# Joining plain loads in a planned graph kernel: adjacency in pairs of tiles, masks once, rows of several lists together

## The chip, the cores and the metric

The kernel runs on one core of one Trainium2 chip. The metric is the device time of one execution in microseconds (us). The kernel before has four runs, and one more execution was taken with the hardware profiler, whose lines are shown below.

## The reference, cut to what matters

There are 16 graphs ("batches") of 1024 nodes with 64 channels, a weighted adjacency of 1024 x 1024 per graph, and a node mask. Layer 0 is a normalised matrix product. Layer 1 takes, for each node and channel, a weighted sum of three quantiles over its neighbours, after some neighbours have been dropped, and then a small MLP.

```python
# layer 0
h = jnp.maximum(_layernorm(x), 0.0)
deg = jnp.clip(jnp.sum(adj, axis=2, keepdims=True), 1.0, None)
x = x + jnp.matmul(adj / deg, h)
# layer 1
h = jnp.maximum(_layernorm(x), 0.0)
adj_d = _dilate_adj(adj, nodemask)           # drops every skip-th neighbour of nodes with more than 10
agg = _weighted_nanquantile_agg(h, adj_d > 0) # 0.25, 0.5, 0.75 with weights 0.25, 0.5, 0.25
hid = jax.nn.relu((h + agg) @ W1 + b1)
x = x + (hid @ W2 + b2) * nodemask[..., None]
```

The adjacency is sparse and very uneven: a few nodes have up to some 88 neighbours, most have five or fewer. A quantile needs the neighbours' values sorted, per channel.

## The kernel before, in words

**Engines and what they do.** PE (TensorE) transposes and multiplies, ACT (ScalarE) copies out of PSUM, makes signs and normalises, DVE (VectorE) finds neighbours and sorts, POOL (GpSimd) issues indirect gathers and scatters, SP (SyncE) issues the plain transfers, in the order in which they are written to its queue.

**First part, per batch.** `loads` (line 570) has SP load the batch's `x` into `xt`, its mask into `mrow`, and its adjacency in eight tiles of 128 rows into `at` (five buffers). `signs` (610) turns a tile into fp16 signs `sg` on ACT, and `listing` has DVE multiply them by descending column numbers and take the eight largest of each of four segments (MAX8 into `rec`): these are the neighbours' numbers. `transposes` turns the same tile on PE, ACT copies it to `att`, and `products` multiplies `att` with the normalised `h0`. `beginnings` (588) makes `h0`, and writes the node number and mask into the last two columns of `row`. `channels` makes layer 1's normalised values and stores them to the table `tab` in DRAM (SP). `endings` ranks the batch's nodes by their degree, and POOL scatters each node's `row` (own values, residual, neighbour list, node, mask: 164 numbers) to `srt`, so that nodes of like degree lie together.

**Second part, per group of four batches.** `group` reads the sorted lists back (`recs`), drops neighbours, and starts a `Job` (841) for each class of list length. There are ten classes for 31 tiles of nodes: lengths 15, 10, 8, 7 (two tiles), 6, and then 5, 4, 3, 2 and 1 with four to six tiles each. A job has POOL gather the neighbours' rows one list place at a time into `places`, SP load the nodes' own rows into `S` (four buffers), DVE sort by a network of minima and maxima between `places` and `other`, and then, in `layers` (1099), PE, ACT and DVE run the MLP into `y` (six buffers). SP loads the residual into `y` first; POOL scatters the result to the output.

**Third part, long lists.** `long_lists` (1299) takes the 128 nodes at each of the first four ranks (lists of up to 88, 31, 24 and 20), one per partition. SP loads their own rows into `lS`, four loads per list, one for each group.

**What sets the order.** All of these are generators that yield the engine they need next and the time from which they can go on. `Plan` holds a clock for each engine and for the transfers, estimates when each tile is ready and when a buffer is free (`room(name, bufs)`), and always runs the entry that can begin first; ties and priorities come from a rank. A change of a buffer count or of a transfer thus changes the order of everything behind it. Every instruction that goes through the plan has the line 238 in the profile, so that groups are told apart by their tiles. A further path for dense graphs follows the list path; it doesn't run on this input.

Of the kernel before, what the change touches and what calls it, by code (L numbers as in the profile page):

```python
# [243 lines left out]
class Plan:  # L244
# [25 lines left out]
    def room(self, name, bufs):  # L270

        tiles = self.slots.get(name, ())
        if len(tiles) < bufs:
            return 0.0
        old = tiles[-bufs]
        return INF if self.users[old] else max(self.used.get(old, 0.0), self.ready.get(old, 0.0))

    def at(self, *tiles):
        return max(self.ready.get(t.tensor.name, INF) for t in tiles)
# [104 lines left out]
def list_path(ctx, tc, x, adj, nodemask, w1, b1, w2, b2, out, go):  # L384
# [93 lines left out]
    wt0 = consts.tile([P, 1], F32, name="wt0")  # L478
    nc.vector.memset(wt0, QUANTILES[0][1])

    before = consts.tile([P, NT], F32, name="before")
    nc.vector.tensor_scalar(before, col_f[:, :NT], -float(P), None, op0=OP.mult)

# [82 lines left out]
    def known(st, *names):  # L566

        return max(at(st[name]) if name in st else INF for name in names)

    def loads(pool, now):  # L570
        def nodes(st, b):
            yield "SP", lambda: room("xt", 3)
            st["xt"] = new(pool, [P, NT, C], F32, "xt", 3, users=1)
            nc.sync.dma_start(st["xt"], x[b].rearrange("(t p) c -> p t c", p=P))
            st["mrow"] = new(tiny, [NT, P], U8, "mrow", 3)
            nc.sync.dma_start(st["mrow"], nodemask[b].rearrange("(t p) -> t p", p=P))

        yield from nodes(batch[0], 0)
        for b, st in enumerate(batch):
            now[0] = b  # L580
            for t in range(NT):
                if t == 2 and b + 1 < B:
                    yield from nodes(batch[b + 1], b + 1)
                yield "SP", lambda: room("at", 5)
                st["rows"][t] = new(pool, [P, N], F32, "at", 5, users=2)
                nc.sync.dma_start(st["rows"][t], adj[b, t * P:(t + 1) * P, :])

    def beginnings(pool, now):

        for b, st in enumerate(batch):  # L590
            now[0] = b
            yield "DVE", lambda: max(known(st, "xt", "mrow"), room("h0", 3), room("row", 4))
            mrow_f = new(tiny, [NT, P], F32, "mrow_f", 2)
            nc.vector.tensor_copy(mrow_f, st["mrow"])

            h0 = new(pool, [P, NT, C + 1], F32, "h0", 3, users=2)
            nc.vector.memset(h0[:, :, C:], 1.0)
            row = st["row"] = new(pool, [P, NT, RW], F32, "row", 4, users=1)
            nc.vector.memset(row[:, :, C:W], -1.0)
            yield from normed(h0[:, :, :C], st["xt"])  # L600
            st["h0"] = h0
            yield "PE", lambda: max(at(mrow_f), room("ps_small", 3))
            pm = new(ps_s, [P, HALF], F32, "ps_small", 3, users=1)
            nc.tensor.transpose(pm[:, :NT], mrow_f, ident[:NT, :NT])
            yield "ACT", lambda: at(pm)
            nc.scalar.copy(row[:, :, RW - 1], pm[:, :NT])
            nc.scalar.copy(row[:, :, RW - 2], row_f)
            free(pm)

    def signs(pool, now):  # L610
        for b, st in enumerate(batch):
            now[0] = b
            for t in range(NT):
                yield "ACT", lambda: max(
                    at(st["rows"][t]) if t in st["rows"] else INF, room("sg", 4),
                    0.0 if t else room("total", 4),
                )
                if t == 0:
                    st["total"] = new(tiny, [P, NT], F32, "total", 4, users=1)
                sg = new(pool, [P, N], HF, "sg", 4, users=1)  # L620
                nc.scalar.activation(
                    sg, st["rows"][t], AF.Sign, accum_out=st["total"][:, t:t + 1]
                )
                st["signs"][t] = sg
                free(st["rows"][t])
# [202 lines left out]
    def scatter(dst, src, idx, others):  # L828
# [9 lines left out]
        others.append(ins.ins)  # L838
        plan.last = others

    class Job:

        def __init__(self, pool, n, T, keys, idx, node, mask, nodes_i, table, S, g, name="places",
                     bufs=4, rank=0, half=False, begin=0.0):
            self.__dict__.update(locals())
            self.short = pool is gat
            self.tag = "" if self.short else "l0" if name == "lplaces0" else "l"
            self.block = BLOCK if self.tag == "l0" else n  # L850
            self.bufs1 = 1 if self.tag == "l0" else 2

        def run(self):
            n, T, pool, short = self.n, self.T, self.pool, self.short

            since = []
            own = () if short else (lambda rank: self.rank,)
            pace = lambda: since[0] + 1.3 * len(since) if not short else 0.0
            yield "POOL", lambda: max(
                self.begin, at(self.idx), room(self.name, self.bufs), room("S", 4) if short else 0.0  # L860
            ), *own
            A = self.A = new(pool, [P, n, T, W], F32, self.name, self.bufs, users=1)
            progress["ahead"] += T * (n - 1)
            parts = self.parts() if self.block < n else None
            if short:
                mine = self.S
                self.S = new(pool, [P, T, C], F32, "S", 4, users=1)
                nc.sync.dma_start(self.S, mine[:, :, :C])
                self.residual = mine[:, :, X1:R0]
            for t in range(T):  # L870
                for k in range(n - 1):
                    if t or k:
                        yield "POOL", pace, *own
                    since.append(since[0] if since else plan.clock["POOL"])
                    plan.own = plan.clock["POOL"]
                    gather(A[:, k + 1, t, :], self.table, self.idx[:, t, k:k + 1])
                    plan.own = None
                    progress["ahead"] -= 1
                    if parts and ((k + 2) % self.block == 0 or k == n - 2):
                        plan.add(parts(), self.rank)  # L880
            if parts:
                yield "DVE", lambda: self.landed if self.left == 0 else INF, self.soon
                yield from self.merge()
                return
            yield "DVE", lambda: max(
                at(A, self.S) + SLACK,
                *(room(self.tag + name, self.bufs1) for name in ("gone", "wu")),
            ), self.soon
            yield from self.sort()
# [209 lines left out]
        def layers(self, terms, sources):  # L1099

            T, R = self.T, terms[0][0].shape[1]
            yield "PE", lambda: max(at(*sources) + LOOSE, room("y", 6), room("pt", 2))
            y = new(mlp, [P, T, CO], F32, "y", 6, users=1)
            x1 = y
            if self.short:
                nc.sync.dma_start(x1, self.residual)
            else:
                x1 = self.S[:, :, X1:R0]
            for t0 in range(0, T, 4):
                ts = range(t0, min(t0 + 4, T))  # L1110
# [51 lines left out]
    def group(g, kept=grp, name=""):  # L1162
# [120 lines left out]
        for t in range(begin, NTAU):  # L1283
            if classes and caps[t] == caps[classes[-1][0]]:
                classes[-1].append(t)
            else:
                classes.append([t])
        for i, ts in enumerate(classes):
            n, T = caps[ts[0]] + 1, len(ts)
            sl = slice(ts[0], ts[-1] + 1)  # L1290
            job = Job(
                gat, n, T, keys[:, sl, :n - 1], idx[:, sl, :], node[:, sl], mask[:, sl],
                nodes_i[:, sl], table, tiles[:, sl, :R0], g,
                half=0 in ts, begin=dropped,
            )
            plan.add(job.run(), 100 * g + i)
        progress["groups"] = g + 1

    def long_lists(pool):

        yield "DVE", always
        rev = new(pool, [P, N], HF, "rev", 1)
        nc.vector.tensor_scalar(rev, col_f, -1.0, float(N), op0=OP.mult, op1=OP.add)
        for l in LORDER:
            K = LONG[l]
            n = K + 1
            yield "SP", always
            S = new(pool, [P, 1, RW], F32, "lS", 4)
            for g in range(NG):
                lo, num = FIRST[g] * LSUB, GROUPS[g] * LSUB  # L1310
                at0 = l * num + (0 if GROUPS[g] == 4 else HP)
                nc.sync.dma_start(
                    S[lo:lo + num, 0, :], srt[g][at0:at0 + num, :]
                )
            node = S[:, 0, RW - 2:RW - 1]
            mask = S[:, 0, RW - 1:RW]
            yield "DVE", lambda: at(S) + SLACK if progress["begun"] == NG else INF
# [377 lines left out]
```

## Time and profile before

| | us |
|---|---|
| median of four runs | 1907.45 |
| the four runs | 1901.99, 1930.16, 1892.49, 1912.90 |
| the profiled execution's own time | 1901.99 |
| its span from the first to the last instruction | 1899.9 |
| DVE busy / POOL busy / PE busy | 1269.7 / 964.8 / 811.9 |
| PE weight loads / ACT busy | 505.8 / 580.0 |

The mean granted clock of TensorE was 0.642 of full speed. In a line of instructions the columns are start, duration, engine, source line, operation, tile written and read, count. In a line of waits they are: who waited, for whom, us in total, how many times, longest. The profile has 16 DMA engines on which the transfers of all queues run; the adjacency is 128 loads of 512 KB, `S` and `y` are 40 loads each, `lS` 16 of 20.5 KB, the mask 16 of 1 KB.

### The profile page before, as it was taken

What the parts mean: (1) busy time and instruction counts of PE and PEld (TensorE: products, weight loads), DVE (VectorE), ACT (ScalarE), POOL (GpSimd) and SP (SyncE); (2) the same over time, 40 slices, a digit from 0 to 9 for tenths busy, and PEclk for the clock granted to TensorE, in tenths of its full rate; (3) what the DMA queues carried; (4) which work ended last, traced back from release to release, by engine and by line L of the source; (5) the groups of instructions that cost most, each with busy time, mean ns of one, the idle gap of its engine ahead of it and who ended that gap; (6) DMA issues with size and microseconds to landing.
All of it is one profiled execution on the core that took longest, in us unless ns stands there. A gap on an engine that the chain in (4) does not pass through costs nothing.

```text
span 1899.9 us, 14970 instructions
## 1 busy us (share of the span) xinstructions
PE 811.9 (43%) x3192; PEld 505.8 (27%) x3192; DVE 1269.7 (67%) x4220; ACT 580.0 (31%) x1746; POOL 964.8 (51%) x1154
## 2 busy tenths in 40 slices
PE   5777743336646435466732643101002003332346
PEld 3333322214423313233422321101001003332334
DVE  7766845958565557457746855778887359695773
ACT  7987743326513313364342341000000000010001
POOL 0123156373455363625667455566787743716654
PEclk8887866565766566677755876555555555765556
DMA  5545644224433212334331222211111100101110
GB/s 163 162 122 148 188 108 109 75 42 113 111 82 78 54 41 74 90 113 105 107 97 47 62 50 52 57 42 43 26 23 25 26 15 9 29 11 37 32 23 15
DMA packets 135710, 133.28 MB, mean 70 GB/s; under 512 B 100756, under 2 KB 103444, under 8 KB 135492
## 3 DMA queue, kind: packets, MB, share of 16 engines
q1 hardware_dynamic: 102876, 90.79, 17.4%
q0 software_dynamic: 32736, 41.47, 9.9%
q14 instruction: 71, 0.58, 0.1%
q8 instruction: 27, 0.44, 0.1%
HBM read 112.90 MB, written 23.61 MB: 72 GB/s over the span
## 4 chain that ended last, share of the span: by engine, by line
DVE 42%; another core or an unknown queue 15%; issue 13%; PE 11%; ACT 11%; DMA 5%; POOL 2%; SPq 0%; DVEq 0%; POOLq 0%; ACTq 0%
PE ps_small L238 6%; DVE places L238 6%; DVE other L238 6%; DVE lplaces L238 5%; PE pt L238 5%; DVE l0other L238 3%; DMA at<-in_adj_dram 3%; ACT sg L238 3%; ACT ln_sq L238 3%; DVE rec L238 2%; ACT att L238 2%; DVE lfound L238 2%; DVE lkey L238 2%; DVE lother L238 2%
## 5 line engine op out<-in xcount | busy, mean ns | idle before, releaser
L238 POOL DMA_INDIRECT places<-tab,idx x372 | 365.8, 983 | 168.8 <-issue 109.1
L238 PE MATMUL pt<-ident,prod 128*128 128x128 f32 (+1 forms) x736 | 165.4, 389 | 528.5 <-DVE prod L238 479.2
L238 PE MATMUL pt<-ident,at 128*128 128x128 f32 x1024 | 200.7, 349 | 268.4 <-issue 127.6
L238 PE MATMUL ps_small<-att,h 128*65 128x512 f32 x512 | 265.7, 670 | 42.7 <-ACT h L238 19.6
L238 PEld LDWEIGHTS pt<-ident,prod 128*128 128x128 f32 (+1 forms) x736 | 134.0, 269 | 562.0 <-issue 337.4
L238 POOL DMA_INDIRECT srt<-row,to x128 | 128.1, 1000 | 285.1 <-ACT row L238 263.5
L238 PEld LDWEIGHTS pt<-ident,at 128*128 128x128 f32 x1024 | 152.4, 179 | 320.8 <-issue 166.6
L238 ACT COPY att<-pt 128x512 f32<-128x512 f32 x256 | 144.3, 582 | 251.0 <-remote 137.1
L238 POOL DMA_INDIRECT lplaces<-whole,lidx x163 | 168.1, 1031 | 49.7 <-issue 49.4
L238 DVE MAX8 rec<-sg 128x8 f16<-128x256 f16 x512 | 180.1, 414 | 8.1 <-remote 2.7
L238 POOL DMA_INDIRECT out_dram<-y,nodes_i x93 | 100.0, 1075 | 156.5 <-DVE y L238 81.5
L238 ACT COPY ot<-pt 128x128 f32<-128x128 f32 (+3 forms) x56 | 22.3, 398 | 447.9 <-PE pt L238 225.8
L238 POOL DMA_INDIRECT places<-tab,last_idx x124 | 123.7, 998 | 53.9 <-issue 36.9
L238 ACT ACTIVATE sg<-at 128x1024 f16<-128x1024 f32 x128 | 134.8, 1054 | 43.9 <-DMA at<-in_adj_dram 23.5
L238 DVE TENSOR_TENSOR sg<-sg,keyed 128x1024 f16<-128x1024 f16 x128 | 87.5, 683 | 73.3 <-ACT sg L238 65.1
L238 PEld LDWEIGHTS ps_small<-att,h 128*65 128x65 f32 x512 | 77.9, 158 | 188.3 <-issue 145.2
L238 PE MATMUL ps_small<-ot,w_sb 128*128 128x128 f32 (+3 forms) x112 | 58.0, 612 | 132.9 <-ACT ot L238 73.0
L238 DVE TENSOR_TENSOR other<-places,other 128x64 f32<-128x64 f32 (+6 forms) x204 | 69.5, 341 | 41.1 <-remote 17.0
L238 DVE TENSOR_TENSOR places<-places,other 128x64 f32<-128x64 f32 (+2 forms) x208 | 62.3, 309 | 22.3 <-remote 7.6
L238 ACT ACTIVATE wu<-wu 128x39 f32<-128x39 f32 (+9 forms) x40 | 9.3, 234 | 197.7 <-DVE wu L238 167.4
L238 DVE TENSOR_TENSOR places<-other,places 128x128 f32<-128x128 f32 (+5 forms) x160 | 54.9, 343 | 19.0 <-DVE other L238 6.8
L238 DVE TENSOR_TENSOR other<-other,places 128x64 f32<-128x64 f32 (+3 forms) x156 | 50.1, 321 | 21.8 <-remote 6.6
(251 smaller groups left out, 1650.7 us busy)
## 6 DMA issues: line engine op xcount, KB each, us to landing
at<-in_adj_dram SPq DMA_DIRECT2D x128, 512.0 KB
places<-tab,idx POOLq DMA_INDIRECT x372
whole<-tab SPq DMA_DIRECT2D x4, 1057.0 KB
tab<-row SPq DMA_DIRECT2D x16, 264.0 KB
xt<-in_x_dram SPq DMA_DIRECT2D x16, 256.0 KB
lplaces<-whole,lidx POOLq DMA_INDIRECT x163
srt<-row,to POOLq DMA_INDIRECT x128
places<-tab,last_idx POOLq DMA_INDIRECT x124
```

Of the source, the lines that this page charges most:

```text
L238: ins = getattr(self._engine, op)(*args, **kwargs)
```

## The change

The adjacency is loaded in pairs of tiles into three buffers of two tiles (before: five of one tile). The masks of all batches are loaded and transposed once at the start, and node numbers and masks are kept in `marks`, from which one ACT copy per batch fills the two columns of `row`. The five classes with lists of more than 5 places (six tiles) share one load of `S` and one of `y`. The four long lists' own rows are loaded by four transfers, one for each group, instead of sixteen. To make room, `sg` has three buffers instead of four and `h0` two instead of three.

```diff
--- before.py
+++ after.py
@@ -478,6 +478,19 @@
     wt0 = consts.tile([P, 1], F32, name="wt0")
     nc.vector.memset(wt0, QUANTILES[0][1])
 
+    mrow = consts.tile([B * NT, P], U8, name="mrow")
+    nc.sync.dma_start(mrow, nodemask.rearrange("b (t p) -> (b t) p", p=P))
+    mrow_f = grp.tile([P, N], F32, name="gat_rows", bufs=1)[:B * NT, :P]
+    nc.vector.tensor_copy(mrow_f, mrow)
+    pm = ps_s.tile([P, HALF], F32, name="ps_small")
+    nc.tensor.transpose(pm[:, :B * NT], mrow_f, ident[:B * NT, :B * NT])
+    marks = consts.tile([P, B, NT, 2], HF, name="marks")
+    nc.vector.tensor_copy(
+        marks[:, :, :, 1].rearrange("p b t -> p (b t)"), pm[:, :B * NT]
+    )
+    nc.vector.tensor_copy(
+        marks[:, :, :, 0], row_f.unsqueeze(1).to_broadcast([P, B, NT])
+    )
     before = consts.tile([P, NT], F32, name="before")
     nc.vector.tensor_scalar(before, col_f[:, :NT], -float(P), None, op0=OP.mult)
 
@@ -572,8 +585,6 @@
             yield "SP", lambda: room("xt", 3)
             st["xt"] = new(pool, [P, NT, C], F32, "xt", 3, users=1)
             nc.sync.dma_start(st["xt"], x[b].rearrange("(t p) c -> p t c", p=P))
-            st["mrow"] = new(tiny, [NT, P], U8, "mrow", 3)
-            nc.sync.dma_start(st["mrow"], nodemask[b].rearrange("(t p) -> t p", p=P))
 
         yield from nodes(batch[0], 0)
         for b, st in enumerate(batch):
@@ -581,43 +592,39 @@
             for t in range(NT):
                 if t == 2 and b + 1 < B:
                     yield from nodes(batch[b + 1], b + 1)
-                yield "SP", lambda: room("at", 5)
-                st["rows"][t] = new(pool, [P, N], F32, "at", 5, users=2)
-                nc.sync.dma_start(st["rows"][t], adj[b, t * P:(t + 1) * P, :])
+                if t % 2 == 0:
+                    yield "SP", lambda: room("at", 3)
+                    pair = new(pool, [P, 2, N], F32, "at", 3, users=4)
+                    nc.sync.dma_start(
+                        pair, adj[b, t * P:(t + 2) * P, :].rearrange("(k p) j -> p k j", p=P)
+                    )
+                st["rows"][t] = pair[:, t % 2, :]
 
     def beginnings(pool, now):
 
         for b, st in enumerate(batch):
             now[0] = b
-            yield "DVE", lambda: max(known(st, "xt", "mrow"), room("h0", 3), room("row", 4))
-            mrow_f = new(tiny, [NT, P], F32, "mrow_f", 2)
-            nc.vector.tensor_copy(mrow_f, st["mrow"])
-
-            h0 = new(pool, [P, NT, C + 1], F32, "h0", 3, users=2)
+            yield "DVE", lambda: max(known(st, "xt"), room("h0", 2), room("row", 4))
+            h0 = new(pool, [P, NT, C + 1], F32, "h0", 2, users=2)
             nc.vector.memset(h0[:, :, C:], 1.0)
             row = st["row"] = new(pool, [P, NT, RW], F32, "row", 4, users=1)
             nc.vector.memset(row[:, :, C:W], -1.0)
             yield from normed(h0[:, :, :C], st["xt"])
             st["h0"] = h0
-            yield "PE", lambda: max(at(mrow_f), room("ps_small", 3))
-            pm = new(ps_s, [P, HALF], F32, "ps_small", 3, users=1)
-            nc.tensor.transpose(pm[:, :NT], mrow_f, ident[:NT, :NT])
-            yield "ACT", lambda: at(pm)
-            nc.scalar.copy(row[:, :, RW - 1], pm[:, :NT])
-            nc.scalar.copy(row[:, :, RW - 2], row_f)
-            free(pm)
+            yield "ACT", lambda: at(row)
+            nc.scalar.copy(row[:, :, RW - 2:], marks[:, b, :, :])
 
     def signs(pool, now):
         for b, st in enumerate(batch):
             now[0] = b
             for t in range(NT):
                 yield "ACT", lambda: max(
-                    at(st["rows"][t]) if t in st["rows"] else INF, room("sg", 4),
+                    at(st["rows"][t]) if t in st["rows"] else INF, room("sg", 3),
                     0.0 if t else room("total", 4),
                 )
                 if t == 0:
                     st["total"] = new(tiny, [P, NT], F32, "total", 4, users=1)
-                sg = new(pool, [P, N], HF, "sg", 4, users=1)
+                sg = new(pool, [P, N], HF, "sg", 3, users=1)
                 nc.scalar.activation(
                     sg, st["rows"][t], AF.Sign, accum_out=st["total"][:, t:t + 1]
                 )
@@ -838,12 +845,14 @@
         others.append(ins.ins)
         plan.last = others
 
+    mine_of = lambda share: share["rows"].shape[1]
+
     class Job:
 
 
 
         def __init__(self, pool, n, T, keys, idx, node, mask, nodes_i, table, S, g, name="places",
-                     bufs=4, rank=0, half=False, begin=0.0):
+                     bufs=4, rank=0, half=False, begin=0.0, shared=None, first=0):
             self.__dict__.update(locals())
             self.short = pool is gat
             self.tag = "" if self.short else "l0" if name == "lplaces0" else "l"
@@ -857,16 +866,23 @@
             own = () if short else (lambda rank: self.rank,)
             pace = lambda: since[0] + 1.3 * len(since) if not short else 0.0
             yield "POOL", lambda: max(
-                self.begin, at(self.idx), room(self.name, self.bufs), room("S", 4) if short else 0.0
+                self.begin, at(self.idx), room(self.name, self.bufs),
+                room("S", 4) if short and not (self.shared and "S" in self.shared) else 0.0,
             ), *own
             A = self.A = new(pool, [P, n, T, W], F32, self.name, self.bufs, users=1)
             progress["ahead"] += T * (n - 1)
             parts = self.parts() if self.block < n else None
             if short:
-                mine = self.S
-                self.S = new(pool, [P, T, C], F32, "S", 4, users=1)
-                nc.sync.dma_start(self.S, mine[:, :, :C])
-                self.residual = mine[:, :, X1:R0]
+                mine, share = self.S, self.shared
+                if share is None:
+                    share = {"users": 1, "rows": mine}
+                if "S" not in share:
+                    S = share["S"] = new(
+                        pool, [P, mine_of(share), C], F32, "S", 4, users=share["users"]
+                    )
+                    nc.sync.dma_start(S, share["rows"][:, :, :C])
+                self.share = share
+                self.S = share["S"][:, self.first:self.first + T, :]
             for t in range(T):
                 for k in range(n - 1):
                     if t or k:
@@ -1099,12 +1115,20 @@
         def layers(self, terms, sources):
 
             T, R = self.T, terms[0][0].shape[1]
-            yield "PE", lambda: max(at(*sources) + LOOSE, room("y", 6), room("pt", 2))
-            y = new(mlp, [P, T, CO], F32, "y", 6, users=1)
-            x1 = y
+            yield "PE", lambda: max(
+                at(*sources) + LOOSE, room("pt", 2),
+                0.0 if self.short and "y" in self.share else room("y", 6),
+            )
             if self.short:
-                nc.sync.dma_start(x1, self.residual)
+                share = self.share
+                if "y" not in share:
+                    y = share["y"] = new(
+                        mlp, [P, mine_of(share), CO], F32, "y", 6, users=share["users"]
+                    )
+                    nc.sync.dma_start(y, share["rows"][:, :, X1:R0])
+                y = x1 = share["y"][:, self.first:self.first + T, :]
             else:
+                y = new(mlp, [P, T, CO], F32, "y", 6, users=1)
                 x1 = self.S[:, :, X1:R0]
             for t0 in range(0, T, 4):
                 ts = range(t0, min(t0 + 4, T))
@@ -1285,6 +1309,9 @@
                 classes[-1].append(t)
             else:
                 classes.append([t])
+        few = [ts for ts in classes if caps[ts[0]] > 5]
+        front = slice(few[0][0], few[-1][-1] + 1)
+        shared = {"users": len(few), "rows": tiles[:, front, :R0]}
         for i, ts in enumerate(classes):
             n, T = caps[ts[0]] + 1, len(ts)
             sl = slice(ts[0], ts[-1] + 1)
@@ -1292,6 +1319,7 @@
                 gat, n, T, keys[:, sl, :n - 1], idx[:, sl, :], node[:, sl], mask[:, sl],
                 nodes_i[:, sl], table, tiles[:, sl, :R0], g,
                 half=0 in ts, begin=dropped,
+                **(dict(shared=shared, first=ts[0] - few[0][0]) if ts in few else {}),
             )
             plan.add(job.run(), 100 * g + i)
         progress["groups"] = g + 1
@@ -1301,17 +1329,18 @@
         yield "DVE", always
         rev = new(pool, [P, N], HF, "rev", 1)
         nc.vector.tensor_scalar(rev, col_f, -1.0, float(N), op0=OP.mult, op1=OP.add)
+        yield "SP", always
+        own_rows = new(pool, [P, len(LONG), RW], F32, "lS", 1)
+        for g in range(NG):
+            lo, num = FIRST[g] * LSUB, GROUPS[g] * LSUB
+            nc.sync.dma_start(
+                own_rows[lo:lo + num, :, :],
+                srt[g][:len(LONG) * num, :].rearrange("(l r) w -> r l w", l=len(LONG)),
+            )
         for l in LORDER:
             K = LONG[l]
             n = K + 1
-            yield "SP", always
-            S = new(pool, [P, 1, RW], F32, "lS", 4)
-            for g in range(NG):
-                lo, num = FIRST[g] * LSUB, GROUPS[g] * LSUB
-                at0 = l * num + (0 if GROUPS[g] == 4 else HP)
-                nc.sync.dma_start(
-                    S[lo:lo + num, 0, :], srt[g][at0:at0 + num, :]
-                )
+            S = own_rows[:, l:l + 1, :]
             node = S[:, 0, RW - 2:RW - 1]
             mask = S[:, 0, RW - 1:RW]
             yield "DVE", lambda: at(S) + SLACK if progress["begun"] == NG else INF
```

## The prediction

> **What bounds the kernel now.** I read the page first, then the stages, then the waits, then SP's own queue.
>
> ```profile
> span 1899.9 us, 14970 instructions
> PE 811.9 (43%) x3192; PEld 505.8 (27%) x3192; DVE 1269.7 (67%) x4220; ACT 580.0 (31%) x1746; POOL 964.8 (51%) x1154
> ...
> DVE 42%; another core or an unknown queue 15%; issue 13%; PE 11%; ACT 11%; DMA 5%; POOL 2%; SPq 0%; DVEq 0%; POOLq 0%; ACTq 0%
> ```
>
> No engine is full over the span. DVE carries the chain most often, and 28% of the chain is waiting that the profile can't name. So I split the span: until the fourth batch is sorted (190 us), until the last batch is (the last `srt` scatter starts at 1178.3), and the tail.
>
> ```profile
> 0.00:190.00 190.00, 130.41 (x514) 69.51 (x514) 134.33 (x475) 155.31 (x472) 37.31 (x72) 0.84 0.51 149
> 190.00:1180.00 990.00, 502.40 (x1884) 299.01 (x1882) 622.85 (x2122) 387.71 (x1175) 504.98 (x630) 0.67 0.33 85
> 1180.00:1900.00 720.00, 179.08 (x796) 137.29 (x796) 512.50 (x1623) 36.96 (x99) 422.55 (x453) 0.56 0.14 28
> ```
>
> The columns are PE, PEld, DVE, ACT, POOL busy, clock, DMA share, GB/s. First ACT is nearly full (155.3 of 190). In the middle DVE is 63% busy and everyone waits in order for someone. In the tail DVE is 71% busy and SP has little to do. Next, the waits of the middle stage (190 to 1180), SP's queue and then DVE:
>
> ```profile
> SPq L238 <- PE pt L238: 138.2, 48, 12.2
> SPq L238 <- DMA out_dram<-y,nodes_i: 103.3, 13, 25.1
> ...
> SPq L238 <- DVE other L238: 40.2, 9, 12.5
> SPq L238 <- DVE places L238: 36.4, 8, 9.6
> SPq L238 <- ACT prod L238: 28.2, 2, 27.8
> ```
> ```profile
> DVE sg L238 <- ACT sg L238: 47.8, 6, 15.9
> ```
>
> SP issues in order. The first line is an adjacency load waiting for a buffer that PE still transposes from. The other four, 208 us, are largely `y` and `S` loads waiting for a buffer: `y` is released by a scatter to the output, `S` by DVE's passes and ACT's copy into `prod`. An adjacency load behind one of them waits too. The timeline of SP shows a case:
>
> ```profile
> 935.03 0.33 SPq L238 DMA_DIRECT2D at<-in_adj_dram  x1
> 955.83 6.97 SPq L238 DMA_DIRECT2D y<-srt  x2
> 963.61 0.01 SPq L238 DMA_DIRECT2D S<-srt  x1
> 965.04 0.01 SPq L238 DMA_DIRECT2D tab<-row  x1
> 966.45 14.41 SPq L238 DMA_DIRECT2D at<-in_adj_dram  x5
> ```
>
> For 31 us no adjacency went out. What that can cost is the DVE line above: listing stood 47.8 us in this stage, in six waits, for a sign that ACT had not made.
>
> **The start.** The changed program puts the mask load, a cast and two copies into `marks` ahead of DVE's first work, and its instruction order has PE transpose the first tile (eight transposes) before the mask rows. The first tile is used at 11.3 us now, the second at 13.1 (PE's 16 transposes run from 11.37 without a gap); a pair lands as a whole, so 13.1 bounds it. Then eight transposes (half of the 3.69 us that 16 took), a mask transpose (0.22), two copies (0.3 together), and then the `keyed` operations (1.5) and the row sums (0.8) that ran at 6.3 to 8.6 before. DVE's first listing moves from 12.4 to about 18, 6 us; ACT's first `ln_sq` from 17.3 to about 18.3. DVE was 76% and ACT 85% busy in the first 100 us, so part is made up: between 0 and +6, I take **+3**.
>
> **The masks.** Out go 16 SP loads (0.32 each), 16 DVE casts (0.207, together 3.3 us), 16 PE transposes (0.22, together 3.5), and one of two small ACT copies per batch (0.18, together 2.9). The SP loads are short and the rest is paid only where its engine is on the chain: 42% of 3.3 and 11% of 6.4 make 2.1. Bounds 0 and -10; I take **-2**.
>
> **Adjacency in pairs.** 128 loads of 512 KB become 64 of 1 MB into three buffers of two tiles instead of five of one. At the best slice's 163 GB/s a tile takes 3.2 us, so the first tile of a pair comes that much later. ACT stood for an adjacency load in 12 of 128 loads (23.5 us in the span); the same share of 64 pairs is 6 stalls, +19 us at 3.2 each; all 12 would be +38. Against it: at 104 us SP stands at `tab<-row`, the adjacency behind it goes out at 106.8, and ACT idles 3.7 us to 112.0. In the new SP order the first four `tab` stores have 12, 12, 14 and 12 more tiles ahead of them than the rows they store, before 11, 9, 10 and 10, so that three such gaps close: -11. Holding time says the same balance: a batch took 38.6 us, 4.8 per tile, so five buffers allow 24 us from load to last transpose; three pairs allow 29, and need some 5 more (3.2 to land, about 2 for the second tile's transposes). Bounds -28 (the 7.1 us that ACT idles in each of the first four batches) and +38; I take **+8**. `sg` falls from 4 buffers to 3 and `h0` from 3 to 2 to pay for the sixth tile. ACT waited 14.1 us in all, 8 times, for a sign buffer; I leave that at nothing here, covered by DVE listing promptly, and price its loss as a rival.
>
> **Own rows and residuals of five lists.** `S` and `y` loads go from 40 each to 24 each. The bytes and the 256-byte pieces stay. A group now takes 6 `y` buffers, all there are, so each load waits for a scatter of a whole group earlier, where ten into six made it wait for one six jobs back. At least the share of loads that disappears, 40%, should go from the 208 us, that is 83 us of SP; but only listing's 47.8 us can be on the path, so 40% of that: **-19**, bounds 0 and -48. The `S` buffer of five lists is held until the fifth is copied; the four `places` buffers bound the jobs in flight anyway, so I count nothing for it.
>
> **Long lists' rows.** 16 loads become 4. They went out from 1181.7 to 1197.3, while DVE was making `last_keys`, which is the chain there; `lnodes` started at 1188.8 already. **0**, bounds -3 and +3: the first list now waits for the rows of all four.
>
> **The order.** Buffers and load times feed the planner, which writes out another order. Counted in it: before the last batch's sorting positions are ready, DVE runs 17 more passes of sorting (696 against 679, 8,448 elements more, some 500 each, 0.69 us by the row of 512), and POOL issues 338 gathers instead of 322. That is 12 us of DVE work moved out of a tail where DVE is 71% busy, into a stage where it idles 37%: between -8 and -12, **-10**. How the 28% unnamed waiting falls in another order no row tells. I give it 0, and for the range the longest such piece of the chain, 27 us, either way.
>
> **Sum.** +3 -2 +8 -19 +0 -10 = -20, on the profiled execution's 1901.99 us (span 1899.9, 2.1 around it): **1882**. That execution lies 0.3% under the median of 1907.45; the four runs go from 1892.49 to 1930.16, and I take about 1% as what a measurement can tell from no change.
>
> [...] The row: an SP load's issue takes 0.32 us, and most loads lie under other work. [...]
>
> **Rivals.**
> (A) *Listing loses its cover, slower.* With three `sg` buffers ACT, which runs in order, stands at a sign until DVE has listed the third tile back, and the copies into `att` behind it stand too, then PE, then the adjacency buffers. One listing is 2.1 us (0.68 + 4 x 0.35); 96 tiles of the last twelve batches make 200 us if every one stands, and with 30%, ACT's busy share of the span, +60: 1882 + 60 = **1942**. For it: ACT already waits for `rec` before a sign at 378 to 384 us, 0.67 each time. Against: only 14.1 us in all. It decides the sign from a third of that, some 20 us on the path; ACT's wait before `sg` for `rec` would then pass 40 us.
> (B) *The transfers were hidden anyway.* Listing's 47.8 us come from ACT standing at `att` copies, not from SP; the -19 is gone, the rest is -1: **1901**. For it: most tiles wait 15 to 50 us for PE after they land.
> (C) *SP was the brake.* The 47.8 us go wholly and the first batches take 35 us instead of 38.6: 1882 - 29 - 14 = **1839**. Against: PE's transposes lag anyway.
> That the change doesn't do what it says is excluded for the counts, since the built order has them; that `y` still blocks SP is B.
>
> **How the numbers follow.** Forecast 0.36, A 0.30, B 0.24, C 0.10. The forecast lies 1% under the profiled run, so a fifth of it falls within 1%, and some of B and A falls to either side: faster 0.41, same 0.24, slower 0.35. The likeliest case's own range is 1855 to 1909 (27 either way); the range reaches to C and A: 1838 to 1945.
>
> **What would show it.** Start: DVE's first `sg` at 17 to 19 us. Pairs: batches one to four still 37 to 40 us apart. Joined loads: in the middle stage SP's wait for `out_dram` under 50 us and DVE's wait for `sg` under 35. Order: the last `srt` scatter within 15 us of 1178, the tail 8 to 12 us shorter. I am wrong if ACT's waits for `rec` pass 40 us, if the middle stage grows, or if the tail grows: the new order would then decide, not the transfers.

## The result, and the profile after

The changed kernel takes 1908.03 us (median of 22 runs, 1893.55 to 1928.43), the kernel before 1913.57 us (32 runs, 1866.34 to 1943.48) beside it. The ratio is 1.0123 (95% interval 1.0080 to 1.0166): slower by 1.2%, where 1% faster was forecast. It compares, as every ratio below does, only the runs within 1.5% of the fastest of each kernel, which are 20 of the 22 runs after but only the 7 lowest of the 32 before, the profiled one not among them. The medians of all runs differ by -0.3%, so how much slower it is, and whether at all, isn't settled. Either way the 20 us are not there. The profiled execution after took 1912.55 us, 10.6 more than the one before.

The page of the kernel after, its first lines and its chain:

```profile
span 1910.8 us, 14597 instructions
...
PE 784.1 (41%) x3177; PEld 487.0 (25%) x3177; DVE 1265.5 (66%) x4207; ACT 577.2 (30%) x1730; POOL 965.6 (51%) x1157
...
DVE 48%; issue 15%; another core or an unknown queue 13%; PE 9%; ACT 9%; POOL 3%; DMA 3%; SPq 0%; DVEq 0%; POOLq 0%; ACTq 0%
```

DVE's work is 4 us less, and the unnamed 28% of the chain ("issue" and "another core or an unknown queue") are still 28%. The stages, cut again at 190 us and at the last `srt` scatter (1181); columns as before:

```profile
0.00:190.00 190.00, 134.31 (x547) 71.50 (x547) 138.68 (x489) 162.42 (x486) 36.57 (x72) 0.90 0.54 161
190.00:1181.00 991.00, 477.29 (x1870) 283.73 (x1870) 625.32 (x2125) 380.24 (x1150) 517.99 (x639) 0.67 0.31 83
1181.00:1910.80 729.80, 172.47 (x760) 131.78 (x760) 501.50 (x1595) 34.50 (x94) 411.01 (x447) 0.55 0.13 28
```

The first stage does more (DVE 138.7 us of work in 190, before 134.3): the fifth batch's sorting positions (tile `to`) come at 187.4 us instead of 198.9. The last `srt` scatter starts at 1181 all the same, so the middle gave the 11 us back and some 3 more. The tail holds 11 us less DVE work (501.5 against 512.5), and cut at the starts of the two scatters, 1180.9 and 1178.3, it is 8.3 us longer (729.9 against 721.6), not 10 shorter.

The waits of the middle stage, SP's queue and then DVE:

```profile
SPq L238 <- PE pt L238: 272.1, 30, 35.0
SPq L238 <- ACT row L238: 97.1, 11, 24.0
SPq L238 <- remote: 76.4, 4, 41.9
...
SPq L238 <- DVE other L238: 42.5, 5, 31.0
...
SPq L238 <- DMA out_dram<-y,nodes_i: 17.7, 6, 6.7
```
```profile
DVE ln_v L238 <- ACT ln_sq L238: 73.8, 6, 47.9
DVE ln_v L238 <- ACT ln_v L238: 35.3, 3, 34.7
DVE sg L238 <- issue: 28.0, 2, 24.5
DVE sg L238 <- ACT sg L238: 16.5, 4, 6.8
```

Before the change DVE's standing ahead of `sg` had an unnamed line too, beside the 47.8 us:

```profile
DVE sg L238 <- issue: 8.2, 1, 8.2
```

The named waits did what was forecast for the joined loads: SP's 103.3 us for `out_dram` fell to 17.7, and DVE's wait for a sign from 47.8 to 16.5. But with the unnamed lines DVE's standing ahead of `sg` fell only from 56.0 to 44.5, and the time did not follow. DVE now stands for other things, 73.8 us for `ln_sq` (before 19.7), 47.9 of them at once. The timeline of that case:

```profile
935.07 0.17 DVE L238 TENSOR_SCALAR ln_s<-ln_s 128x8 f32<-128x8 f32 x1
...
935.40 0.95 POOL L238 DMA_INDIRECT places<-tab,idx  x1 [0.30 <-issue]
...
952.90 0.95 POOL L238 DMA_INDIRECT places<-tab,idx  x1 [0.31 <-issue]
953.63 0.59 ACT L238 COPY ot<-pt 128x512 f32<-128x512 f32 x1 [25.82 <-remote]
...
964.13 0.69 ACT L238 ACTIVATE hid<-ps_small,b_sb 128x512 f32<-128x512 f32 x1 [9.92 <-issue]
```
```profile
983.20 0.17 DVE L238 TENSOR_SCALAR ln_v<-ln_v 128x8 f32<-128x8 f32 x1 [47.95 <-ACT ln_sq L238]
```

ACT stands 25.8 us for a transpose into `pt` that PE had finished at about 930, and nothing in the profile says for what. Meanwhile POOL issues gathers back to back, 0.95 us each and 0.30 us apart. Such standing is all over the trace. I counted it: a run is POOL's gathers and scatters starting less than 2 us apart; its late part is all that comes more than 16 us after its start; standing is DVE's gaps over 0.3 us from 190 us on.

| | us in late parts of runs | DVE stood there | elsewhere |
|---|---|---|---|
| before | 497 | 266 | 245 in 1213 us |
| after | 527 | 329 | 197 in 1194 us |

In a late part DVE stands 0.53 us of each us before and 0.62 after, elsewhere 0.20 and 0.17. It sets in with time: in the runs of the kernel before DVE stands 0.15 us per us in the first 16 us, 0.40 from 16 to 24 us, 0.58 from 24 to 32 and 0.66 later. The kernel after stands 63 us more in late parts and 48 us less elsewhere, some 15 us more in all. Each row is a single execution, and those of the unchanged kernel lie up to 77 us apart in one and the same order; 15 us, or the 8 of the tail, are less than that.

### The profile page after: what moved, and what is told of

It reads as the page before. It is cut to its first block, busy times and chain, and to the rows that moved or that the text cites. A ratio compares the mean times of both kernels' runs of the same rounds, so it can differ in the third digit from the quotient of the medians.

```text
span 1910.8 us, 14597 instructions
## 1 busy us (share of the span) xinstructions
PE 784.1 (41%) x3177; PEld 487.0 (25%) x3177; DVE 1265.5 (66%) x4207; ACT 577.2 (30%) x1730; POOL 965.6 (51%) x1157
## 4 chain that ended last, share of the span: by engine, by line
DVE 48%; issue 15%; another core or an unknown queue 13%; PE 9%; ACT 9%; POOL 3%; DMA 3%; SPq 0%; DVEq 0%; POOLq 0%; ACTq 0%
DVE places L238 7%; DVE other L238 7%; DVE lplaces L238 6%; PE ps_small L238 5%; DVE rec L238 4%; PE pt L238 3%; DVE l0other L238 3%; ACT sg L238 2%; ACT ln_sq L238 2%; DVE sg L238 2%; DVE lother L238 2%; POOL places L238 2%; ACT att L238 1%; DVE lkey L238 1%
## 5 line engine op out<-in xcount | busy, mean ns | idle before, releaser
L238 PE MATMUL pt<-ident,prod 128*128 128x128 f32 (+1 forms) x736 | 156.0, 373 | 535.6 <-DVE prod L238 324.5
L238 PEld LDWEIGHTS pt<-ident,prod 128*128 128x128 f32 (+1 forms) x736 | 128.3, 257 | 565.4 <-issue 504.6
L238 PE MATMUL pt<-ident,at 128*128 128x128 f32 x1024 | 189.6, 335 | 149.8 <-ACT att L238 64.1
L238 POOL DMA_INDIRECT out_dram<-y,nodes_i x93 | 94.0, 1011 | 236.8 <-DVE y L238 170.8
L238 PEld LDWEIGHTS pt<-ident,at 128*128 128x128 f32 x1024 | 143.7, 171 | 204.5 <-issue 103.8
L238 POOL DMA_INDIRECT lplaces<-whole,lidx x163 | 164.1, 1007 | 49.7 <-issue 49.1
L238 POOL DMA_INDIRECT places<-tab,last_idx x124 | 134.5, 1085 | 67.8 <-issue 36.9
L238 ACT ACTIVATE sg<-at 128x1024 f16<-128x1024 f32 x128 | 134.3, 1051 | 45.7 <-DMA at<-in_adj_dram 24.6
L238 ACT ACTIVATE hid<-ps_small,b_sb 128x128 f32<-128x128 f32 (+2 forms) x56 | 28.2, 504 | 139.6 <-PE ps_small L238 59.6
L238 PE MATMUL ps_small<-w_sb,hid 128*128 128x64 f32 x256 | 55.4, 364 | 31.9 <-ACT hid L238 19.7
```

What stands on the lines that cost most here:

```text
L238: ins = getattr(self._engine, op)(*args, **kwargs)
```

## The experiments

**Conditions.** Here one thing has to be known to read the numbers: on four of the five chips that the experiments ran on, the kernel before takes 1491 us, not 1914; on the fifth, the last three experiments, it takes 1945.5. Each ratio is against the kernel before on the same chip. Each chip was used at one time only, so chip and time can't be told apart.

**The kernel before, unchanged, at 1491 us.**

> The kernel before, unchanged, for a profile under the conditions of the experiments, where it takes 1491 us instead of 1907. T2's rival to the waits that the profile could not name (28% of the chain): if they belong to the conditions and not to the kernel's order, the last srt scatter comes near 900 us instead of 1178, DVE stands in long runs of POOL's gathers less than 0.06 us per us instead of 0.31 to 0.41, and its unnamed waits go. If they belong to the order, they are here too, in the same places.

1489.21 us, ratio 0.9996 (0.9974 to 1.0019). Its stages (the last `srt` scatter at 893.3):

```profile
0.00:190.00 190.00, 139.74 (x573) 74.18 (x574) 143.81 (x506) 168.47 (x516) 37.04 (x72) 0.88 0.53 163
190.00:893.30 703.30, 443.81 (x1826) 262.45 (x1823) 610.79 (x2091) 371.25 (x1133) 510.56 (x629) 0.75 0.42 116
893.30:1484.20 590.90, 176.01 (x796) 136.00 (x796) 509.88 (x1625) 36.84 (x99) 438.49 (x454) 0.57 0.15 35
```

The program is the same and DVE's work (1264.5 us) nearly so; DVE is idle 220 us (1484.2 - 1264.5) instead of 630 (1899.9 - 1269.7). In the late parts of POOL's runs it stands 50 us in 738, 0.07 per us. So most of DVE's idle time belongs to the conditions; a good half of the difference in standing, 216 of 407 us, lay in these late parts. At 1491 us DVE is 85% busy.

**Each part alone, on the kernel before.**

```diff
 # pairs: with three buffers of two tiles, sg 4 to 3, h0 3 to 2
-                yield "SP", lambda: room("at", 5)
+                if t % 2 == 0:
+                    yield "SP", lambda: room("at", 3)
```

> Only the adjacency in pairs (three buffers of two tiles, sg 4 to 3, h0 3 to 2); the rest is the kernel before. T1, the transfers' direct effects add up: the early batches come 35 us apart instead of 38.6 (11 us by the fifth sorting positions), and the time is 5 to 15 us below before. T2, the order that the planner writes decides: the early batches still come 35 us apart, but the whole moves by some 10 us to either side, and the 11 us are not found at the last srt scatter.

1499.61 us, 1.0061 (1.0038 to 1.0083): slower. The fifth sorting positions come at 188.7 us, in the kernel before under these conditions at 182.2. Its early batches come 31 to 39 us apart already, so there is no early gain to be had.

```diff
 # masks
-            nc.scalar.copy(row[:, :, RW - 1], pm[:, :NT])
-            nc.scalar.copy(row[:, :, RW - 2], row_f)
+            nc.scalar.copy(row[:, :, RW - 2:], marks[:, b, :, :])
```

> Only the masks loaded once ahead of the first listing. T1: DVE's first sg at 16 to 18 us instead of 12.4, then 2 us gained: within 0.3% of before. T2: 48 small instructions fewer move the planner's order as much as any other part: the time moves by up to 1% either way though nothing large is removed.

1492.46 us, 1.0011 (0.9987 to 1.0036): no difference.

```diff
 # rows and residuals of five lists
-                nc.sync.dma_start(x1, self.residual)
+                    nc.sync.dma_start(y, share["rows"][:, :, X1:R0])
```

> Only the own rows and residuals of five lists joined (32 transfers fewer). T1: SP's wait for the output's scatters (103 us in the middle stage) goes, DVE's wait for sg falls from 48 to under 35, and the time is 10 to 19 us lower. T2: the SP waits change their names (to pt and row), DVE's wait moves to another tile, and the time is within 10 us of before.

1490.81 us, 1.0001 (0.9980 to 1.0023): no difference, as the second theory has it. There was little to gain here: in the middle stage DVE waits 13.0 us for a sign without the joined loads and 14.2 with them. And each of these three parts writes an order of its own, so that the ratios hold a part's effect and its order's together.

```diff
 # long lists' rows
-            for g in range(NG):
-                nc.sync.dma_start(S[lo:lo + num, 0, :], srt[g][at0:at0 + num, :])
+            S = own_rows[:, l:l + 1, :]
```

> Only the long lists' rows in 4 loads instead of 16, late in the program. T1: 0, within 3 us. T2: the tail's order changes with the load times that the planner sees; the stages before the last srt scatter stay within 3 us of before, and the tail moves by some us either way.

1492.49 us, 1.0007 (0.9985 to 1.0030). DVE's and POOL's instruction order is the same as before here, so that this is the part's own effect: none.

**All parts together, at 1491 us.**

> The changed kernel, all parts together, under the same conditions. T1, effects add up: the parts alone gave 1.0061, 1.0011, 1.0001 and 1.0007, so 1.008, some 1503 us. T2, the order decides: the four parts together write an order of their own, anything between 0.99 and 1.02 and not the product.

1485.04 us, 0.9960 (0.9942 to 0.9978), where the product of the parts is 1.008. The effects don't add up.

```profile
190.00:912.00 722.00, 444.20 (x1877) 267.98 (x1875) 627.24 (x2135) 376.51 (x1150) 525.14 (x639) 0.75 0.41 115
912.00:1487.20 575.20, 169.63 (x760) 130.82 (x760) 494.28 (x1589) 34.67 (x94) 422.51 (x447) 0.56 0.15 35
```

DVE's tail has 15.6 us less work than before and is 15.7 us shorter; the middle has 16.4 us more work and is 18.7 us longer. The work was moved, and found no idle time to lie in: DVE is idle 94.8 us in the middle (722.0 - 627.2), before 92.5.

**The order alone.** No transfer and no buffer changes here:

```diff
-SLACK = 2.0
+SLACK = 2.2
```

> The kernel before with the planner's constant SLACK at 2.2 instead of 2.0: the same instructions in another order, no transfer changed. T1: within 0.2%. T2: the order alone moves the time by 0.3% or more to either side, as much as any part of the change.

1517.10 us, 1.0179 (1.0150 to 1.0209). A 10% larger constant of the planner costs more than any part of the change brings or takes.

**The buffers paid for the pairs.**

```diff
-                sg = new(pool, [P, N], HF, "sg", 4, users=1)
+                sg = new(pool, [P, N], HF, "sg", 3, users=1)
-            h0 = new(pool, [P, NT, C + 1], F32, "h0", 3, users=2)
+            h0 = new(pool, [P, NT, C + 1], F32, "h0", 2, users=2)
```

First with the planner's counts (`room("sg", 3)`, `room("h0", 2)`) lowered too:

> The kernel before with only sg from 4 to 3 buffers and h0 from 3 to 2; the adjacency stays in single tiles, so no transfer changes. Theory P1, the pairs lose by the buffers taken for them: ratio 1.005 or more, ACT waits for rec before sg. Theory P2, they lose by landing late or by the order: within 0.2% of before.

1528.55 us, 1.0261 (1.0231 to 1.0291). Then the two halves of it apart. Only the real buffers, DVE's and POOL's order as before (ACT's moved, by up to 87 places):

> The kernel before, its planner still counting sg in 4 and h0 in 3 buffers, so that DVE's and POOL's instruction order is that of before; the pools really hold 3 and 2. P1, the missing buffers cost directly: most of the 38 us that both edits together cost (1.0261) are here, ratio 1.015 or more. P3, the order that the planner writes for fewer buffers costs: within 0.4% of before.

1507.79 us, 1.0112 (1.0075 to 1.0149). Only the planner's counts, the real buffers as before:

```diff
-                    at(st["rows"][t]) if t in st["rows"] else INF, room("sg", 4),
+                    at(st["rows"][t]) if t in st["rows"] else INF, room("sg", 3),
-            yield "DVE", lambda: max(known(st, "xt", "mrow"), room("h0", 3), room("row", 4))
+            yield "DVE", lambda: max(known(st, "xt", "mrow"), room("h0", 2), room("row", 4))
```

> The reverse: the planner counts sg in 3 and h0 in 2 buffers, so that DVE's and POOL's order is that of the run with fewer buffers (1.0261), but the pools really hold 4 and 3 as before. P1: back within 0.5% of before. P3: 1.02 or more, since the order stays. If both are near 1.013 the two share it.

1533.97 us, 1.0286 (1.0250 to 1.0322). So the whole loss is in the order: in it, the real buffers make no difference (1.0286 with all of them, 1.0261 with fewer). In the order of before, which was written for four and three, the missing buffers, and the order of ACT that comes with them, cost 1.1%: the fifth sorting positions come at 206.3 us instead of 182.2, and 17 of those 24 us are left at the end.

**Rival A in the changed kernel: four sign buffers again.**

```diff
-                sg = new(pool, [P, N], HF, "sg", 3, users=1)
+                sg = new(pool, [P, N], HF, "sg", 4, users=1)
```

> The changed kernel with DVE's and POOL's order as it is, but four real sg buffers instead of three (the mask tile moves into another one's space for it). Rival A of the prediction, listing lost its cover: 1% or more below the changed kernel's 0.996. Otherwise within 0.3% of it: ACT waited 20 us for rec before sg in both kernels.

1492.23 us, 1.0005 (0.9983 to 1.0026), against 0.9960 with three: no gain, if anything a loss. POOL's order is the same, DVE's but for seven lines; ACT's moved by 1.5 places on average. With `room("sg", 4)` in the planner too:

> The same with the planner counting four sg buffers too: another order. T1: as the run with four real buffers and the old order, within 0.3%. T2: it differs from that run by 0.5% or more to either side, with the same instructions and the same buffers.

1497.74 us, 1.0029 (1.0000 to 1.0059). This and the run before it overlap, though they are two orders: not every order can be told from another. Rival A is not what ails the changed kernel here.

**More transfers, the order kept.** The kernel before with

```diff
+                tc.nc.sync.dma_start(extra[k:k + 1, :], w1[0:1, :16])
```

behind each adjacency load:

> The kernel before with 128 further transfers on SP, of 64 bytes each, one issued for each adjacency load into a tile that nobody reads; the planner does not see them, so DVE's and POOL's order is that of before. SP issues 408 transfers instead of 280, by 0.32 us each 41 us more of its time. B, transfers are hidden: within 0.4% of before. C, SP is the brake: 1.01 or more.

1489.35 us, 0.9996 (0.9974 to 1.0017). All 128 were issued between 5.7 and 164.3 us, 0.25 us each, so 32 us more of SP's time in the stage where ACT is nearly full (168.5 of 190 us in the kernel before at 1491 us) cost nothing. They say nothing on the middle stage, where none fell.

**The changed kernel without pairs, and in another order.** Without:

```diff
-                if t % 2 == 0:
-                    yield "SP", lambda: room("at", 3)
+                yield "SP", lambda: room("at", 5)
```

> The changed kernel with the adjacency back in single tiles (five buffers, sg 4, h0 3); masks, joined rows and residuals, and long lists' rows as changed. Effects add up: the three parts alone gave 1.0011, 1.0001 and 1.0007, so 1.002. The order decides: anything between 0.99 and 1.02, and no relation to 0.996 for all four.

1492.47 us, 1.0021 (1.0005 to 1.0037): here the parts do add up, which may be chance, each being in an order of its own. With `SLACK = 2.2`:

> The changed kernel with the planner's SLACK at 2.2 instead of 2.0: the same transfers, another order. If the changed kernel's 0.996 belongs to its transfers, it stays within 0.3% of 0.996; if to its order, it moves by 0.5% or more, to either side (on the kernel before the same edit cost 1.8%).

1496.59 us, 1.0039 (1.0015 to 1.0063), 0.8% above 0.9960 with the same transfers. The 0.4% that the changed kernel gains at 1491 us hangs on its order: in this one the same transfers lose 0.4%.

**Long runs of gathers broken, where the kernel before takes 1945.5 us.** The kernel before with

```diff
+        gathers.append(0)
+        if len(gathers) % 10 == 0:
+            for _ in range(6):
+                tc.nc.gpsimd.memset(rest, 0.0)
```

in `gather`, DVE's order unchanged:

> The kernel before with six memsets of one column on POOL behind every tenth gather, unseen by the planner: DVE's order is kept, POOL's long runs of gathers are broken, at some 2 us each. H1, long runs of gathers make hand-offs late: under the conditions of the first comparison (1908 us) DVE's standing in runs of 16 us and more falls from 0.31 to 0.41 us per us to under 0.15 and the time falls by over 3%. H2, the late hand-offs belong to those conditions and a run of gathers harms nothing by itself: at 1490 us, where DVE stands 0.04 to 0.05 us per us in such runs, nothing is gained, and POOL's 120 us more cost between 0 and 3%.

1855.89 us, 0.9645 (0.9540 to 0.9751); by the medians of all runs 0.954. 396 instructions more on POOL make the kernel 3.5% faster. Six of them take 0.90 us, not the 2 us that I expected:

```profile
1436.93 0.90 POOL L831 MEMSET rest<- 128x1 f32 x6
```

Its stages after 190 us:

```profile
190.00:1187.60 997.60, 485.73 (x1878) 288.11 (x1876) 623.02 (x2122) 385.91 (x1172) 524.72 (x821) 0.68 0.31 84
1187.60:1861.60 674.00, 194.17 (x796) 143.19 (x796) 511.86 (x1623) 36.76 (x99) 449.53 (x658) 0.56 0.14 31
```

Against the profile of before (taken in the first comparison, where that kernel ran in 1902 us; there is no profile of it from this chip) the tail is 48 us shorter, with the same work; the middle has not gained. The price of a long run was forecast to fall under 0.15 and did not: in late parts DVE stands 186 us in 398, 0.47 per us. Late parts became rarer, 398 us instead of 497, and 80 us of standing went with them; 39 us came back elsewhere (284 in 1274 us). The difference, 41, is near that of the spans, 38. But a pause leaves the starts of two gathers about 2 us apart (1435.99 and 1437.98 around the one above), just at my limit: with 1.9 us as the limit the late parts are 80 us instead of 483. And in runs counted by 2 us the standing still sets in with time, 0.31 per us from 16 to 24 us and 0.58 from 24 to 32. So the gain is shown, and how the pauses bring it is not.

**The changed kernel in two more orders, same chip.** `SLACK = 1.8`, and then 1.5:

> The changed kernel with SLACK at 1.8 instead of 2.0, another order of the same transfers. If 0.996 is the transfers' own, 0.993 to 0.999; if the order decides, anything from 0.985 to 1.02. If it lies under 0.996 it is the version that beats both.

1987.39 us, 1.0384 (1.0305 to 1.0462); by the medians of all runs 1.022.

> The same with SLACK at 1.5: one more order, on the same terms; a constant a third lower than the one that the kernel has should write a worse order if 2.0 was well chosen: above 1.00.

1988.34 us, 1.0284 (1.0125 to 1.0443), again 1.022 by the medians. Both lie above the 1.0039 that another order cost at 1491 us; DVE stands 338 and 359 us in late parts of runs. Neither beats both kernels; the pauses beat the kernel before where hand-offs are late, and were not run where they are not, nor in the changed kernel.

## Why the prediction was wrong

Two terms failed: the 0 for the waits that have no name, and the -19 for the joined rows, which is nearly the whole sum.

*The waits that have no name, in another order: 0, bounds 27 either way.* The profile had 28% of its chain in such waits and I took their sum as a constant. 410 us of DVE's idle time (630 us against 220) come and go with the conditions, a good half of them in the late parts of POOL's runs, and how long a run gets is what a new order can change (497 us in late parts before, 527 after). After the change there were 63 us more of standing in late parts and 48 us less elsewhere; what of this the order did and what differs between any two executions isn't shown. Even without the late hand-offs the bounds were too tight: 27 us are 1.4%, and the order alone moved 1491 us by 1.8 and 2.9%.

*The order, -10 (-8 to -12).* The count was right: 11 us of DVE's work left the tail, at 1491 us 15.6. The reading was wrong twice. I called DVE's 37% idle in the middle a place where work can lie; it is made of waits, and under the experiments' conditions the moved work made the middle longer by as much (16.4 us more work, 18.7 us more time). And in the comparison DVE's idle time in the tail rose by 19 us (729.9 - 501.6 against 721.6 - 512.5), so that it came out 8 longer.

*Joined rows, -19 (0 to -48).* This step failed too: it took 40% of a named wait for time on the path. The named waits went as stated, within the thresholds that I gave, and the time did not. Of the 47.8 us for a sign 31 went, but ahead of `sg` DVE stood only 11.5 us less in all, for `ln_sq` 54 us more, and the middle stage took 990.9 us instead of 988.3. The part alone gave 1.0001 at 1491 us, in its own order and where the wait was small to begin with. So nothing of the 19 us shows, as rival B has it; a size under the conditions of the comparison, with the order held, was not measured. A wait that vanishes is no gain where the same engines find another wait behind it.

*Pairs, +8, and the start, +3.* In the comparison the early batches came 33 to 36 us apart, not 37 to 40, and the two steps together gave -11, inside the bounds of -28 to +44 and on the other side of the value. DVE's first `sg` was at 19.8 us, later than the 17 to 19 that I gave. At 1491 us the loss is there: fifth positions 5.6 us later in the changed kernel, and 1.0061 for pairs alone, in their own order.

*Masks, -2, and long lists' rows, 0.* Neither is contradicted within what can be told (1.0011 and 1.0007); 2 us are too few to see.

*Rival A.* ACT's wait for `rec` before `sg` rose from 14.1 to 17.5 us, far from the 40 that I had set, and a fourth buffer gives nothing back. The kernel before loses 1.1% by the fewer buffers, in its own order.

*Rival B* named the right value for the joined loads and, with 1901, nearly the right time, but not the cause; the last sentence of the prediction had it: if the middle or the tail grows, the new order decides. I gave that no chance of its own. Of what moved the two kernels apart at 1914 us, the standing in late parts of runs is counted; that the order put it there is a reading and not shown, since no experiment held the order there and changed the transfers.

## What to carry to other kernels

Where a planner writes the order, price a change by its order too: nudge one of the planner's constants on the unchanged kernel first, and what that moves (here 1.8%, and 2.9% by its buffer counts) is the least that a forecast must allow for. Add up all lines of waits ahead of an instruction, the unnamed ones too, before calling a wait gone. Idle time that is made of waits is no room for moved work (here 16.4 us of it made the middle 18.7 us longer). Where a large part of the chain has no releaser, look at what the other engines do during it before taking it for a constant.

## What the runs showed of the hardware

**Hand-offs late in POOL's long runs, under some conditions.** At 1914 us even an instruction that follows its own engine's result waits. The groups of two such DVE operations, before in the comparison and then in the experiments at 1491 us; the last column is the idle time before them:

```profile
L238 DVE RECIPROCAL deg<-deg 128x4 f32<-128x4 f32 x32 | 5.7, 178 | 4.4 <-remote 2.3 <-issue 1.1
L238 DVE SCALAR_TENSOR_TENSOR to<-low,pos 128x8 int32<-128x8 int32 x16 | 2.7, 168 | 3.1 <-remote 2.6
```
```profile
L238 DVE RECIPROCAL deg<-deg 128x4 f32<-128x4 f32 x32 | 5.7, 178 | 1.1
L238 DVE SCALAR_TENSOR_TENSOR to<-low,pos 128x8 int32<-128x8 int32 x16 | 2.7, 169 | 0.5
```

The durations (178 and 168 ns) are the same; the excess is two cases of 2.3 and 2.6 us and one of 1.1. The first two come 38 and 33 us after the start of one long run of gathers; here is the case of `to`:

```profile
407.78 0.17 DVE L238 TENSOR_SCALAR low<-low 128x8 int32<-128x8 int32 x1 [1.21 <-issue]
407.86 0.17 DVE L238 TENSOR_SCALAR pos<-pos 128x8 f32<-128x8 f32 x1
410.58 0.17 DVE L238 SCALAR_TENSOR_TENSOR to<-low,pos 128x8 int32<-128x8 int32 x1 [2.56 <-remote]
```

The kernel after has two such cases, of 2.3 and 2.5 us, 41 and 48 us after the start of a run. At 1491 us the 48 operations of the two groups wait 0.034 us each in the kernel before, long run or not. On the fifth chip none of them is late with the pauses, and four are, by 1.6 to 3.1 us, in the changed kernel with `SLACK = 1.5`. Of the five chips of the experiments one shows late hand-offs. The clock is lower there and in the first comparison too (0.63 to 0.66 of full speed against 0.68 to 0.71), and PE was busy 811.9 us instead of 759.6 for the same program, but DVE (1269.7 and 1264.5) and ACT (580.0 and 576.6) were not much longer; 52 us of PE don't make up 410 us of DVE's idle time by themselves.

**Lost records.** The traces of the late kind hold fewer semaphore events: 10,353 in the kernel before, 24,706 for the same program at 1491 us, and in late parts of runs 1.4 to 2.2 recorded landings of transfers per us against 13 to 15. So records are missing there; whether the updates themselves are late too they don't tell. No run was made without the recording.

What stays open is whether the updates or only their records suffer, and why on that chip. That pauses in POOL's gathers gain 3.5% there is shown; how they do so is not.
